# Graph attention layer: queries and values by Strassen's seven products, products that add to a bank behind its reader, softmax later, the end written out

## Chip, cores and metric

One core of a Trainium2 chip. The metric is the device time of one execution in microseconds (us). PE is the matmul engine (TensorE), DVE is VectorE, ACT is ScalarE, SP is the engine that issues DMAs.

## What is computed

The reference passes `x` of 128 graphs x 64 nodes x 256 features (f32) through four layers, each added to its input after a normalisation: graph convolutions with batch normalisation, a spectral layer, graph convolutions with an LSTM over skip windows, and graph attention. The change lies in the fourth. Cut to what matters, with `H` the input after layer normalisation and ReLU:

```
Xq = H @ W_lin.T          # queries, 8192 x 256 by 256 x 256
Xv = H @ W_val.T          # values
e[edge, head] = sum over d of a * leaky_relu(Xq[src] + Xq[dst])  +  log(adj[src, dst] + 1e-8)   # 512 edges, 4 heads, slope 0.2
alpha = softmax of e over the edges that share src
y[src] += alpha * Xv[dst]
out = x + y @ W_out.T
```

## The kernel before

`x` stays in SBUF as 16 blocks `X` of 512 rows (4 row tiles of 128 rows, `TPB`). `layer3` is the fourth layer. It makes 32 steps `g`, each over 4 graphs (half a block); 8 steps form a group that shares one softmax. The tile scheduler decides each engine's order from the order of the code, except in `turn`, where `nc.ordered` fixes it. Every operation goes through a helper, so all have the line L799 in the profile and are told apart by their tiles.

What one step does, in order, and the tiles by which the profile names it:

- `score`: for each of 4 graphs and 2 feature halves a matmul of `Q` (64 rows) with the sum of both edge incidences, `S2` (`ps<-ed_S,Q`), each into one bank; ACT takes it with ReLU into `r` (8 buffers).
- `weighted` of step v-1 (v = g - 10): 16 small matmuls of values `XV` with `an` into `y2`, copied to `y`.
- `reduce`: 8 matmuls of `r` with the attention vector, added into the bank `acc` (`acc<-r,ed_apad`).
- `between` of step v = `spread` (four DVE multiplications of `at` with an edge incidence (`ed_OST`) into `aw`, five buffers) and `gathered` (8 matmuls `ps<-aw,ed_ODT`, copied to `an` by ACT).
- after every eighth step `softmax`: `shifted` first adds the linear part to `acc` by the matmul `acc<-ed_S,lin`, then two scans, a maximum, a subtraction and an exponential (`sm_m`, `sm_e`), then two more scans and a reciprocal on DVE. `edgewise` turns the result into `at` two steps later.
- on odd steps, for the next block, `turned` (normalised `h` by ACT, 8 transposes `ps<-ident,h` into two banks, one copied to `hT` by ACT and one by DVE), then `output`, then `queries`.
- `output` of step v-1: 4 matmuls `ps<-w_o,y`, the residual added by DVE into `X`, and a DMA of 256 KB to `out`.
- in the first eight steps `back` adds transposes `ps<-ident,ls_t` of what the LSTM left.

`queries` multiplies each row tile of `hT` with `WQV`, which holds both weights side by side:

```
for j in range(TPB):
    p = psum.tile([P, BT], F32, name="ps")
    for kc in range(2):
        self.mm(p[:], hT[:, kc, j * P:(j + 1) * P], WQV[:, kc, :], kc == 0, kc == 1)
    self.act(Q[:, j, :], p[:, 0:D], AF.Copy)
    o.copy(V[:, j, :], p[:, D:2 * D])
```

and then forms `lin_p` and its two reductions on DVE. PSUM has five banks named `ps`, one `acc` and two for `y2`. After the 32 steps `turn` holds the last softmax, and a plain loop finishes the last eight `between`, `weighted` and `output`.

Of the kernel before, what the change touches and what calls it, by code (L numbers as in the profile page):

```python
# [8 lines left out]
F32 = mybir.dt.float32  # L9
I32 = mybir.dt.int32  # L10
AF = mybir.ActivationFunctionType
# [12 lines left out]
class Ops:  # L24
# [9 lines left out]
    def add(self, o, a, b):  # L34
        self.tt(o, a, b, ALU.add)
# [807 lines left out]
class Plan:  # L843
# [56 lines left out]
    def rest(self):  # L900

        while any(self.queue.values()):
            for e in self.queue:
                self.fill(e, 1e9)
# [561 lines left out]
class Kernel:  # L1466
# [949 lines left out]
    def layer3(self):  # L2416
        nc, o, io = self.nc, self.o, self.io
        cx, (w,) = self.stage([("l3x", 1)], "tile")
        with cx:
            cy, pools = self.stage([("l3", 2), ("l3v", 2), ("l3s", 1), ("l3r", 6), ("l3ps", 5), ("l3cps", 1), ("l3yps", 1)], "tile")  # L2420
            with cy:
                self.a02 = self.everywhere(w, "ed_a", io["L3_gnn_a"].rearrange("h d -> (h d)"))
                o.ts(self.a02[:], self.a02[:], 0.2, ALU.mult)
                self.drop, self.dropr = (w.tile([P, E], F32, name="ed_" + n) for n in ("drop", "dropr"))
                o.ts(self.drop[:], self.cont[:], 1.0, ALU.subtract, FLOOR, ALU.mult)
                o.ts(self.dropr[:], self.contr[:], 1.0, ALU.subtract, FLOOR, ALU.mult)
                WQV = w.tile([P, 2, 2 * D], F32, name="w3_qv")
                for x, n in enumerate(("W_lin", "W_val")):
                    nc.sync.dma_start(WQV[:, :, x * D:(x + 1) * D],
                                      io[f"L3_gnn_{n}_t"].rearrange("(k p) m -> p k m", p=P))  # L2430
                WO = self.weights(w, "w3_o", io["L3_gnn_W_out_t"])


                st, LAG = {}, 10
                self.turned(st, 0, *pools)
                self.queries(st, 0, WQV, *pools)
                for g in range(8 * NG):
                    v = g - LAG
                    ahead = (g + 1) // 2 if g % 2 and g + 1 < 8 * NG else None
                    self.score(st, g, *pools)  # L2440
                    if v >= 1:
                        self.weighted(st, v - 1, *pools)
                    self.reduce(st, g, *pools)
                    if g % 8 == 1 and 1 < g:
                        self.edgewise(st, g // 8 - 1, *pools)
                    if v >= 0:
                        self.between(st, v, *pools)
                    if g % 8 == 7 and g + 1 < 8 * NG:
                        self.softmax(st, g // 8, *pools)
                    if ahead:  # L2450
                        self.turned(st, ahead, *pools)
                    if g < 8:
                        self.back(8 + g, pools[4], "ps")
                    if g + 6 == 8 * NG:

                        p = pools[4].tile([P, BT], F32, name="ps")
                        for c in range(4):
                            self.nc.tensor.transpose(p[:N, c * P:(c + 1) * P], self.OST[:, c, :], self.ident[:])
                        self.act_copy(self.cont[:N, :], p[:N, :])
                    if v >= 1 and g + 1 < 8 * NG:  # L2460
                        self.output(st, v - 1, WO, *pools)
                    if ahead:
                        self.queries(st, ahead, WQV, *pools)
                self.turn(st, WO, pools)
                for v in range(8 * NG - 8, 8 * NG + 2):
                    if v < 8 * NG:
                        self.between(st, v, *pools)
                    if 8 * NG - 8 < v <= 8 * NG:
                        self.weighted(st, v - 1, *pools)
                    if v > 8 * NG - 7:  # L2470
                        self.output(st, v - 2, WO, *pools)

    def turned(self, st, i, pool, vp, sp, rp, psum, psc, psy):

# [2 lines left out]
        for dc in range(2):  # L2477
# [2 lines left out]
                self.nc.tensor.transpose(p[:, j * P:(j + 1) * P], h[:, j, dc * P:(dc + 1) * P], self.ident[:])  # L2480
            self.move(hT[:, dc, :], p[:])

    def queries(self, st, i, WQV, pool, vp, sp, rp, psum, psc, psy):

        o, hT = self.o, st["hT"]
        Q = rp.tile([P, TPB, D], F32, name="Q", bufs=2)
        V = st["V", i] = rp.tile([P, TPB, D], F32, name="XV", bufs=7)
        st["Q", i] = Q
        for j in range(TPB):
            p = psum.tile([P, BT], F32, name="ps")  # L2490
            for kc in range(2):
                self.mm(p[:], hT[:, kc, j * P:(j + 1) * P], WQV[:, kc, :], kc == 0, kc == 1)
            self.act(Q[:, j, :], p[:, 0:D], AF.Copy)
            o.copy(V[:, j, :], p[:, D:2 * D])

        if i % 4 == 0:
            st["lin", i // 4] = pool.tile([P, 2, 2, 8, HEADS], F32, name="lin")
            self.nc.vector.memset(st["lin", i // 4][:], 0.0)
        lin, pr = st["lin", i // 4], sp.tile([P, TPB, D], F32, name="lin_p")
        o.mul(pr[:], Q[:], self.a02[:, None, :].to_broadcast([P, TPB, D]))  # L2500
        k = 2 * (i % 4)
        for x in range(2):
            s = slice(64 * x, 64 * x + 64)
            o.red(lin[s, x, :, k:k + 2, :].rearrange("p m a h -> p a m h"),
                  pr[s].rearrange("p (a m) (h d) -> p a m h d", m=2, h=HEADS), ALU.add)
# [27 lines left out]
    def turn(self, st, WO, pools):  # L2533


        nc, o, psum = self.nc, self.o, pools[4]
        q, v = NG - 1, 8 * NG - 10
        nc.ordered = True
        W = [self.spread(st, v, c, *pools) for c in (0, 2)]
        e, m, m2 = self.shifted(st, q, *pools)  # L2540
        self.output(st, v - 2, WO, *pools)
        self.gathered(st, v, W, *pools)
        et = m2[:].rearrange("p (c b) -> p c b", c=4)
        p = psum.tile([P, 4, P], F32, name="ps")
        for c in range(4):
            nc.tensor.transpose(p[:, c, :], e[:, c * P:(c + 1) * P], self.ident[:])
        self.act_copy(et, p[:])
        self.weighted(st, v - 1, *pools)
        W = [self.spread(st, v + 1, 0, *pools)]
        p = psum.tile([P, P], F32, name="ps")  # L2550
        for c in range(4):
            self.mm(p[:N, :], self.OST[:, c, :], et[:, c, :], c == 0, c == 3)

        sums = self.contr[:N, 0:P]
        o.ts(sums, p[:N, :], 0.5, ALU.max)
        o.recip(sums, sums)
        self.output(st, v - 1, WO, *pools)
        W.append(self.spread(st, v + 1, 2, *pools))
        self.gathered(st, v + 1, W, *pools)
        at = st["at", q] = pools[1].tile([P, 4, 2, 8, 2, HEADS], F32, name="at")  # L2560
        p = psum.tile([P, 4, P], F32, name="ps")
        for c in range(4):
            self.mm(p[:, c, :], self.cont[:N, c * P:(c + 1) * P], sums)
        for x in range(2):
            for m in range(2):
                z = 64 * x + 32 * m
                by = lambda t: t[:, :, z:z + 32].rearrange("p c (a h) -> p c a h", h=HEADS)
                o.mul(at[:, :, x, :, m, :], by(et), by(p))
        self.weighted(st, v, *pools)
        self.output(st, v, WO, *pools)  # L2570
        self.weighted(st, v + 1, *pools)
        nc.ordered = False
        self.output(st, v + 1, WO, *pools)

    def softmax(self, st, q, pool, vp, sp, rp, psum, psc, psy):

# [7 lines left out]
        o.mul(e[:], e[:], m2[:])  # L2584
        st["e", q] = e

    def shifted(self, st, q, pool, vp, sp, rp, psum, psc, psy):

        nc, o = self.nc, self.o
        acc, lin = st["acc", q], st["lin", q]  # L2590
        self.mm(acc[:], lin[:].rearrange("p x m a h -> p (x m a h)"), self.S2[:], False, True)
        e, m, m2 = (vp.tile([P, E], F32, name="sm_" + x, bufs=1) for x in ("e", "m", "m2"))
        scan = nc.vector.tensor_tensor_scan
        scan(m[:], self.drop[:], acc[:], -FLOOR, op0=ALU.add, op1=ALU.max)
# [58 lines left out]
            (self.move if g < 8 * NG - 11 else self.act_copy)(y[:, :, :, x, :].rearrange("p f m s -> p m f s"),  # L2653
                      yp[:, x, 0:4 * N].rearrange("p (m f s) -> p m f s", m=2, f=2))

    def output(self, st, g, WO, pool, vp, sp, rp, psum, psc, psy):

        y = st["y", g]
        p = psum.tile([P, 2, D], F32, name="ps")
        for m in range(2):  # L2660
            for f in range(2):
                self.mm(p[:, m, :], y[:, f, m].rearrange("p x s -> p (x s)"), WO[:, f, :], f == 0, f == 1)
        x = self.X[g // 2][:, 2 * (g % 2):2 * (g % 2) + 2, :]
        self.o.add(x, x, p[:])
        out = self.io["out"].rearrange("b n d -> (b n) d")
        self.nc.sync.dma_start(out[2 * g * P:(2 * g + 2) * P, :].rearrange("(t p) d -> p t d", p=P), x)

    def run(self):
        self.begin()
# [54 lines left out]
```

## Time and profile before

| | |
|---|---|
| median of 3 runs | 2345.52 us (2345.03 to 2349.55) |
| profiled execution | 2350.61 us, its span 2348.8 us |
| mean granted PE clock | 0.994 of full speed |
| fourth layer in the trace | from about 1750 us to the end |
| PE, DVE, ACT busy | 98%, 68%, 48% of the span |
| largest DMA queue | 7.3% of the time of 16 engines |

The page and the answers of the trace give groups of instructions as engine, operation, out<-in, shape and count, then busy time and mean duration, then idle time ahead of them and what ended it. A matmul of f32 is recorded as two passes. Matmuls overlap in the array, so a group's mean is longer than the distance from one start to the next; distances are taken from the timeline, whose columns are the start, the length, the engine and the group.

### The profile page before, as it was taken

The page shows a single profiled execution, that of the slowest core. Times are in us where ns is not written, and L with a number is a line of the kernel's source. Part 1 is how long each engine was busy: PE and PEld are TensorE (multiplying, and loading weights), DVE is VectorE, ACT ScalarE, POOL GpSimd, SP SyncE. Part 2 cuts the span into 40 slices and gives each one's busy share as a digit, 9 for nine tenths or more (in the row PEclk, how much of TensorE's full clock was granted, in tenths as well). Part 3 has the DMA queues.
Part 4 walks back from the last instruction along what each step waited for, and adds up shares of the span by engine and source line. Part 5 has one row for each costly group of instructions (what it writes and reads, how often), then busy time and mean ns, then how long its engine had stood idle before and what let it go on. Part 6 is the DMA issues. An engine that isn't in the chain of part 4 may idle for free.

```text
span 2348.8 us, 32636 instructions
## 1 busy us (share of the span) xinstructions
PE 2298.7 (98%) x12173; PEld 1633.1 (70%) x12173; DVE 1590.5 (68%) x3988; ACT 1138.2 (48%) x2503; POOL 2.9 (0%) x26
## 2 busy tenths in 40 slices
PE   7999998999999999999999999999999999999999
PEld 4555446986777788888999998888874444444444
DVE  7877676998447777666767667569655566556457
ACT  4665864654436654444444444347445544334321
POOL 0000000000000000000000000000000000000000
PEclk9999999999999999999999999999999999999999
DMA  5000221130010000001000001000020000000001
GB/s 170 1 1 19 63 60 29 66 89 19 1 36 1 1 19 1 1 1 37 1 1 1 1 8 65 1 1 17 1 72 1 1 5 19 14 15 14 19 19 46
DMA packets 61193, 54.86 MB, mean 23 GB/s; under 512 B 15204, under 2 KB 58853, under 8 KB 61029
## 3 DMA queue, kind: packets, MB, share of 16 engines
q1 hardware_dynamic: 61028, 52.73, 7.3%
q8 instruction: 97, 1.59, 0.3%
q14 instruction: 68, 0.55, 0.1%
HBM read 35.93 MB, written 16.78 MB: 22 GB/s over the span
## 4 chain that ended last, share of the span: by engine, by line
PE 80%; DVE 3%; ACT 1%; issue 0%; DMA 0%; ACTq 0%; DVEq 0%
PE ps L799 69%; PE acc L799 5%; PE pt L799 4%; DVE sm_m L799 1%; PE pe L799 1%; PE y L799 1%; DVE X L799 0%; DVE aw L799 0%; ACT ls_g L799 0%; ACT L799 0%; DMA ls_w<-in_L_gnn_Wih_t_dram 0%; DVE ls_g L799 0%; DVE XV L799 0%; DVE ls_t L799 0%; DVE hT L799 0%
## 5 line engine op out<-in xcount | busy, mean ns | idle before, releaser
L799 ACT ACTIVATE ls_g<-ls_g,ls_b 128x512 f32<-128x512 f32 (+4 forms) x472 | 243.0, 565 | 153.4 <-DVE ls_g L799 151.5
L799 ACT ACTIVATE ls_g<-ps,ls_b 128x256 f32<-128x256 f32 (+3 forms) x268 | 115.4, 470 | 330.4 <-PE ps L799 327.1
L799 PE MATMUL ps<-z,w 128*128 128x512 f32 x512 | 259.0, 630 | 0.9 <-ACT z L799 0.9
L799 DVE TENSOR_TENSOR aw<-at,ed_OST 128x1024 f32<-128x1024 f32 x128 | 149.1, 1220 | 97.4 <-PE ps L799 97.4
L799 PE MATMUL ps<-big,X 128*128 128x176 f32 (+3 forms) x848 | 213.0, 367 | 0.8 <-ACT big L799 0.7
L799 DVE TENSOR_TENSOR ls_g<-ls_z,ps 128x512 f32<-128x512 f32 (+5 forms) x256 | 147.1, 580 | 91.4 <-PE ps L799 90.0
L799 PE MATMUL ps<-ls_tx,X 128*128 128x160 f32 (+2 forms) x960 | 207.1, 327 | 0.6 <-ACT ls_g L799 0.6
L799 PE MATMUL ps<-X,X 128*128 128x160 f32 (+1 forms) x896 | 199.1, 306 | 0.0
L799 PE MATMUL ps<-X,ls_w 128*128 128x256 f32 x640 | 190.5, 379 | 0.0
L799 PEld LDWEIGHTS ps<-ls_tx,X 128*128 128x128 f32 x960 | 161.9, 190 | 15.2 <-DVE X L799 4.9
L799 PEld LDWEIGHTS ps<-big,X 128*128 128x128 f32 x848 | 146.1, 190 | 30.5 <-issue 19.4
L799 DVE TENSOR_TENSOR X<-ls_g 128x1024 f32<-128x1024 f32 (+2 forms) x108 | 117.5, 1088 | 51.1 <-ACT ls_g L799 51.1
L799 ACT ACTIVATE r<-ps 128x512 f32<-128x512 f32 x256 | 129.2, 626 | 43.1 <-PE ps L799 43.1
L799 PEld LDWEIGHTS ps<-X,X 128*128 128x128 f32 x896 | 148.5, 190 | 0.0
L799 PE MATMUL ps<-X,ls_s 128*128 128x256 f32 x480 | 142.3, 379 | 0.0
L799 PEld LDWEIGHTS ps<-z,w 128*128 128x128 f32 x512 | 88.7, 193 | 70.9 <-issue 62.3
L799 PE MATMUL ps<-ls_tx,ls_s 128*128 128x256 f32 x464 | 134.9, 379 | 0.0
L799 PE MATMUL ps<-ls_tx,ls_w 128*128 128x256 f32 x464 | 133.4, 380 | 0.0
L799 PEld LDWEIGHTS ps<-X,ls_w 128*128 128x128 f32 x640 | 121.6, 190 | 16.6 <-DVE X L799 0.3
L799 PE MATMUL ps<-big,ls_w 128*128 128x256 f32 x464 | 132.0, 380 | 0.7 <-ACT ls_z L799 0.7
L799 PE MATMUL ps<-ed_S,Q 64*128 64x512 f32 x512 | 129.6, 617 | 2.3 <-DVE XV L799 2.2
L799 ACT ACTIVATE h<-X,n_m,n_r 128x256 f32<-128x256 f32 x192 | 99.6, 590 | 40.9 <-issue 25.0
(543 smaller groups left out, 4010.4 us busy)
## 6 DMA issues: line engine op xcount, KB each, us to landing
X<-in_x_dram SPq DMA_DIRECT2D x32, 512.0 KB
xs<-X SPq DMA_DIRECT2D x16, 512.0 KB
X<-xs SPq DMA_DIRECT2D x16, 512.0 KB
out_dram<-X SPq DMA_DIRECT2D x32, 256.0 KB
X<-in_L_gnn_Wih_t_dram SPq DMA_DIRECT2D x4, 512.0 KB
ls_w<-in_L_gnn_Wih_t_dram SPq DMA_DIRECT2D x4, 512.0 KB
ls_w<-in_L_gnn_Whh_t_dram SPq DMA_DIRECT2D x4, 512.0 KB
w<-in_L_gnn_W_t_dram SPq DMA_DIRECT2D x2, 512.0 KB
```

The lines of the kernel that those rows point to most:

```text
L799: i = method(*a, **kw)
```

## The change

- `queries` multiplies a block of 512 x 256 with the two weights as a 2 x 2 product of 256 x 256 pieces in Strassen's form with seven products (Winograd's variant): each is 2 matmuls of 256 columns. Four stand ahead of `output`, three (`rest`) behind it. Products 2, 4 and 3 have no `start`: they add to the banks a, f and d of products 1, 7 and 5, which by then have been read. `hold` keeps the three behind what PE was given before.
- The outputs are put together by DVE: five additions with an operand in PSUM, and two copies of 512 by ACT.
- `turned` makes three sums (`hS`, one in place in `hT`) right behind the transposes and is moved from the odd step to the even step before; the fourth sum is formed in `queries`. `sums3` makes four sums of the weights once.
- `Q` has one buffer instead of two. The linear part's matmul is a function of its own, `summed`, ahead of the queries; the rest of `softmax` comes after `rest()`.
- In `turn`, `at` is formed ahead of `gathered`, and the last loop is written out in fixed order: half of the next step's `spread` is issued early, the residual additions come a step later (`late`), and the last output goes in two halves, each with its own bank, addition and DMA.

```diff
                 self.turned(st, 0, *pools)
-                self.queries(st, 0, WQV, *pools)
+                WQV = self.sums3(w, WQV)
+                self.queries(st, 0, WQV, *pools)()
...
                     if g % 8 == 7 and g + 1 < 8 * NG:
-                        self.softmax(st, g // 8, *pools)
-                    if ahead:
-                        self.turned(st, ahead, *pools)
+                        self.summed(st, g // 8, *pools)
                     if g < 8:
                         self.back(8 + g, pools[4], "ps")
+                    if ahead:
+                        rest = self.queries(st, ahead, WQV, *pools)
+                    elif g + 2 < 8 * NG:
+                        self.turned(st, g // 2 + 1, *pools)
...
                     if ahead:
-                        self.queries(st, ahead, WQV, *pools)
+                        rest()
+                    if g % 8 == 7 and g + 1 < 8 * NG:
+                        self.softmax(st, g // 8, *pools)
                 self.turn(st, WO, pools)
-                for v in range(8 * NG - 8, 8 * NG + 2):
...
+        A = [[hT[:, k, 256 * t:256 * t + 256] for k in range(2)] for t in range(2)]
+        S = sp.tile([P, 2, 256], F32, name="hS")
+        S1, S2, S3 = A[1][0], S[:, 0], S[:, 1]
+        self.o.sub(S3, A[0][0], A[1][0])
+        self.o.add(S1, A[1][0], A[1][1])
+        self.o.sub(S2, S1, A[0][0])
+        st["sums", i] = A, S1, S2, S3
+
+    def sums3(self, w, WQV):
+        o = self.o
+        B = [[WQV[:, k, D * x:D * x + D] for x in range(2)] for k in range(2)]
+        T1, T2, T3 = (w.tile([P, D], F32, name=f"w3_t{n}")[:] for n in range(3))
+        o.sub(T1, B[1][1], B[0][1])
+        o.sub(B[0][1], B[0][1], B[0][0])
+        o.sub(T2, B[1][1], B[0][1])
+        o.sub(T3, B[1][0], T2)
+        return {1: B[0][0], 2: B[1][0], 3: B[1][1], 5: B[0][1], 7: T1, 6: T2, 4: T3}
...
+        def product(a, m, bank, first):
+            if first:
+                banks[bank] = psum.tile([P, 2, D], F32, name="ps")
+            for u in range(2):
+                nc.tensor.matmul(banks[bank][:, u, :], a[:, u * P:(u + 1) * P], WQV[m], start=first and u == 0,
+                                 stop=u == 1, skip_group_check=True)
+            return banks[bank][:]
+
+        Z, U = V[:, 0:2, :], V[:, 2:4, :]
+        a = product(A[0][0], 1, "a", True)
+        self.act_copy(Z, a)
+        o.add(Z, Z, product(S2, 6, "b", True))
+        o.add(U, Z, product(S3, 7, "f", True))
+
+        o.sub(S3, A[0][1], S2)
+        o.add(U, U, product(S1, 5, "d", True))
+
+        def rest():
+            nc.hold((nc.mark()[0], None, None))
+            self.act_copy(Q[:, 0:2, :], product(A[0][1], 2, "a", False))
+            o.add(Q[:, 2:4, :], Z, product(A[1][1], 4, "f", False))
+            o.add(Z, Z, product(S3, 3, "d", False))
+            nc.hold()
+            self.linear(st, i, pool, vp, sp, rp, psum, psc, psy)
...
         W = [self.spread(st, v, c, *pools) for c in (0, 2)]
+        self.summed(st, q, *pools)
         e, m, m2 = self.shifted(st, q, *pools)
...
-        self.gathered(st, v + 1, W, *pools)
         at = st["at", q] = pools[1].tile([P, 4, 2, 8, 2, HEADS], F32, name="at")
...
+        self.gathered(st, v + 1, W, *pools)
+        W = [self.spread(st, v + 2, 0, *pools)]
         self.weighted(st, v, *pools)
-        self.output(st, v, WO, *pools)
-        self.weighted(st, v + 1, *pools)
+        late = lambda: None
+        for v in range(8 * NG - 8, 8 * NG + 2):
+            if v < 8 * NG:
+                W.append(self.spread(st, v, 2, *pools))
+            late()
+            if v < 8 * NG:
+                self.gathered(st, v, W, *pools)
+            if v + 1 < 8 * NG:
+                W = [self.spread(st, v + 1, 0, *pools)]
+            if v <= 8 * NG:
+                self.weighted(st, v - 1, *pools)
+            late = self.output(st, v - 2, WO, *pools, late=True)
+        late()
         nc.ordered = False
...
+        for lo, hi in ((0, 1), (1, 2)) if g == 8 * NG - 1 else ((0, 2),):
+            p = psum.tile([P, 2, D], F32, name="ps")[:, 0:hi - lo, :]
...
+        def add():
+            for p, lo, hi in parts:
+                x = self.X[g // 2][:, 2 * (g % 2) + lo:2 * (g % 2) + hi, :]
+                self.o.add(x, x, p)
+                self.nc.sync.dma_start(out[(2 * g + lo) * P:(2 * g + hi) * P, :].rearrange("(t p) d -> p t d", p=P), x)
```

More of the change, by code (lines that the diff above doesn't have):

```diff
@@ L2462, in layer3 @@
                     if ahead:
-                        self.queries(st, ahead, WQV, *pools)
+                        rest()
+                    if g % 8 == 7 and g + 1 < 8 * NG:
+                        self.softmax(st, g // 8, *pools)
                 self.turn(st, WO, pools)
-                for v in range(8 * NG - 8, 8 * NG + 2):
[L2466 to L2471, printed above, removed]
     def turned(self, st, i, pool, vp, sp, rp, psum, psc, psy):
@@ L2483, in queries @@
     def queries(self, st, i, WQV, pool, vp, sp, rp, psum, psc, psy):
-        o, hT = self.o, st["hT"]
-        Q = rp.tile([P, TPB, D], F32, name="Q", bufs=2)
+        nc, o, (A, S1, S2, S3) = self.nc, self.o, st["sums", i]
+        Q = st["Q", i] = rp.tile([P, TPB, D], F32, name="Q", bufs=1)
         V = st["V", i] = rp.tile([P, TPB, D], F32, name="XV", bufs=7)
[L2488 to L2494, printed above, removed]
+        banks = {}
@@ new lines, in queries @@
+        o.add(U, Z, product(S3, 7, "f", True))
[8 more added lines that the diff above has]
+            self.linear(st, i, pool, vp, sp, rp, psum, psc, psy)
+        return rest
@@ L2496, in queries, with linear @@
+    def linear(self, st, i, pool, vp, sp, rp, psum, psc, psy):
+        o, Q = self.o, st["Q", i]
         if i % 4 == 0:
@@ L2568, in turn @@
                 o.mul(at[:, :, x, :, m, :], by(et), by(p))
+        self.gathered(st, v + 1, W, *pools)
+        W = [self.spread(st, v + 2, 0, *pools)]
         self.weighted(st, v, *pools)
-        self.output(st, v, WO, *pools)
-        self.weighted(st, v + 1, *pools)
+        late = lambda: None
[11 more added lines that the diff above has]
+        late()
         nc.ordered = False
-        self.output(st, v + 1, WO, *pools)
     def softmax(self, st, q, pool, vp, sp, rp, psum, psc, psy):
@@ L2585, in softmax, with summed @@
         st["e", q] = e
+    def summed(self, st, q, pool, vp, sp, rp, psum, psc, psy):
+        self.mm(st["acc", q][:], st["lin", q][:].rearrange("p x m a h -> p (x m a h)"), self.S2[:], False, True)
     def shifted(self, st, q, pool, vp, sp, rp, psum, psc, psy):
-        nc, o = self.nc, self.o
-        acc, lin = st["acc", q], st["lin", q]
-        self.mm(acc[:], lin[:].rearrange("p x m a h -> p (x m a h)"), self.S2[:], False, True)
+        nc, o, acc = self.nc, self.o, st["acc", q]
         e, m, m2 = (vp.tile([P, E], F32, name="sm_" + x, bufs=1) for x in ("e", "m", "m2"))
@@ L2654, in weighted, with output @@
                       yp[:, x, 0:4 * N].rearrange("p (m f s) -> p m f s", m=2, f=2))
-    def output(self, st, g, WO, pool, vp, sp, rp, psum, psc, psy):
+    def output(self, st, g, WO, pool, vp, sp, rp, psum, psc, psy, late=False):
         y = st["y", g]
[L2659 to L2664, printed above, removed]
-        out = self.io["out"].rearrange("b n d -> (b n) d")
-        self.nc.sync.dma_start(out[2 * g * P:(2 * g + 2) * P, :].rearrange("(t p) d -> p t d", p=P), x)
+        out = self.io["out"].rearrange("b n d -> (b n) d")
+        parts = []
+        for lo, hi in ((0, 1), (1, 2)) if g == 8 * NG - 1 else ((0, 2),):
+            p = psum.tile([P, 2, D], F32, name="ps")[:, 0:hi - lo, :]
+            for m in range(lo, hi):
+                for f in range(2):
+                    self.mm(p[:, m - lo, :], y[:, f, m].rearrange("p x s -> p (x s)"), WO[:, f, :], f == 0, f == 1)
+            parts.append((p, lo, hi))
+        def add():
[3 more added lines that the diff above has]
+                self.nc.sync.dma_start(out[(2 * g + lo) * P:(2 * g + hi) * P, :].rearrange("(t p) d -> p t d", p=P), x)
+        if late:
+            return add
+        add()
     def run(self):
```

## The prediction, made before the result

> **What bounds the kernel now.** I read the page first, then the table by stage, the groups by form from 1750 us on (where the fourth layer begins; it runs to the end at 2348.8, some 597 us), the timelines of a middle step, the waits and the chain.
>
> ```profile
> PE 2298.7 (98%) x12173; PEld 1633.1 (70%) x12173; DVE 1590.5 (68%) x3988; ACT 1138.2 (48%) x2503; POOL 2.9 (0%) x26
> PE 80%; DVE 3%; ACT 1%; issue 0%; DMA 0%; ACTq 0%; DVEq 0%
> ```
>
> PE is busy for 98% of the span and carries 80% of the chain. Busy matmul time alone would not prove that (the Trainium skill, "Trainium Kernel Development and Optimization", warns of it as a metric), so the table by stage follows: time of the stretch, then PE, PEld, DVE, ACT, POOL busy, clock, DMA share, GB/s.
>
> ```profile
> 2050.00:2100.00 50.00, 50.00 (x294) 22.77 (x293) 25.59 (x39) 19.79 (x42) 0.00 (x0) 1.00 0.05 17
> 2250.00:2300.00 50.00, 48.27 (x361) 22.57 (x359) 32.13 (x37) 12.53 (x27) 0.00 (x0) 1.00 0.08 27
> ```
>
> In a middle stretch PE never rests, DVE is half free and ACT 60% free; at the end of the layer PE loses time. So matmul passes taken away count in full as long as DVE and ACT keep up. The groups (busy, mean ns | idle before) and PE's timeline of one odd step give the prices:
>
> ```profile
> L799 PE MATMUL ps<-w_qv,hT 128*128 128x512 f32 x256 | 113.0, 594 | 3.5 <-DVE hT L799 3.5
> L799 PEld LDWEIGHTS ps<-w_qv,hT 128*128 128x128 f32 x256 | 47.7, 190 | 59.3 <-issue 48.5 <-DVE hT L799 5.0 <-PE ps L799 3.3
> L799 DVE TENSOR_TENSOR aw<-at,ed_OST 128x1024 f32<-128x1024 f32 x128 | 149.1, 1220 | 97.4 <-PE ps L799 97.4
> L799 DVE TENSOR_TENSOR X<-X,ps 128x512 f32<-128x512 f32 x48 | 32.2, 682 | 24.9 <-PE ps L799 24.7
> L799 DVE COPY XV<-ps 128x256 f32<-128x256 f32 x64 | 26.5, 416 | 34.1 <-ACT Q L799 34.0
> L799 ACT ACTIVATE Q<-ps 128x256 f32<-128x256 f32 x64 | 24.4, 381 | 62.7 <-PE ps L799 62.3
> L799 ACT ACTIVATE r<-ps 128x512 f32<-128x512 f32 x256 | 129.2, 626 | 43.1 <-PE ps L799 43.1
> ```
> ```profile
> 2237.04 1.09 PE L799 MATMUL ps<-ident,h 128*128 128x128 f32 x8
> 2237.97 1.89 PE L799 MATMUL ps<-w_o,y 128*128 128x256 f32 x8
> 2239.70 7.03 PE L799 MATMUL ps<-w_qv,hT 128*128 128x512 f32 x16
> 2246.66 3.91 PE L799 MATMUL ps<-ed_S,Q 64*128 64x512 f32 x16
> ```
>
> An f32 matmul is two passes. The matmul means overlap, so starts are used: 16 passes of 512 from 2239.70 to 2246.66 are 6.96 us, 0.429 each and 0.09 for the change to the 64-row score. The w_o passes of 256 are 8 in 1.73 us: 0.216 each, exactly half, although a weight load takes 0.190.
>
> **What the Trainium skill says.** "TensorE: Matmul & The Clock Gate", Back-to-back issue gap: spacing in a stream of load and matmul is set by both. The w_o row agrees that at 256 columns the load (0.190) still fits below the pass (0.216), with 0.026 to spare. The same page, What's actually happening: about 3.4 us of idling halves the clock. This trace has it once: a stage at 0.97 (2000 to 2050) after a softmax whose stalls add up. "PSUM — Partial Sum Buffer", The four PSUM rules: a synchronised read in the middle of an accumulation group is allowed, so products that add to a bank behind its reader must wait for the reader; no run here shows that yet.
>
> **The change, part by part.** The sum is against the profiled execution (2350.6, a span of 2348.8 and 1.8 around it). That run is 5.1 above the median of 2345.5; I take the difference in both alike.
>
> 1. Products. Per block of 512 rows 8 matmuls of 512 (16 passes, 6.96) become 14 of 256 (28 x 0.216 + 0.09 = 6.15): -0.81, and x16 blocks **-12.9**. w_o moves between the fourth and the fifth product and ident,h ahead of the w_o of the step before; both change neighbours but not the number of changes between tile shapes, so nothing.
>
> 2. Copies and adds. Three of the sums go with hT into the even step before, where PE wants them only 11 us later; the fourth and the adds follow the products. Per block DVE loses 4 XV copies (1.66) and gains 5 adds out of PSUM (5 x 0.68) and 4 sums of 256 (4 x 0.42): +3.4; ACT goes from 4 x 0.38 to 2 x 0.60. Laid out from the start of an odd score: score 3.9, y 0.6, acc 3.5, aw 3.5, so the products start at +11.5 and the first four end at +15.0, w_o at +16.7. DVE finishes its four aw at about +14.5, then adds: Z +15.2, U +15.9, the last sum +16.3, U +17.0, X +17.7. The fifth product (bank a) waits for ACT alone, the sixth (from +17.6) for U at +15.9, the seventh (from +18.4) for the sum and U at +17.0. About 1.4 us to spare: the adds are hidden by w_o and the fifth and sixth products. If that cover were gone they would cost up to 2.4 a block. Queued behind them on DVE are the adds to Q and Z, lin_p and its two reductions; the next score needs the banks that Q and Z are read from, free by about +20, against its fourth and sixth tiles at that time: margin 0.1. After the even step the sixth score tile waits for the X add, 0 to 0.15: +0.1 x 9 = **+0.9**.
>
> 3. ACT. In blocks 1 to 6 the normalisation (h, four of 0.59) now no longer lies below the 7 us of w_qv, since `turned` comes before w_o of the even step; it mixes with the eight r of the next score, which pace that score's banks (8 r take 4.03 against 3.9 for the matmuls). I read from the order of instructions that an r waits behind one or two h: 0.5 to 0.85 each, **+3.9** for six.
>
> 4. First block. No step runs ahead of it: its sums queue behind the last LSTM work on DVE (ls_g, X, big; done about 1757.9 in the timeline of DVE), and Z and U come after. The block, which ended at 1760.8, ends at about 1763: **+2.3**. The four sums of weights (4 x 0.42) come earlier, below LSTM matmuls: nothing; if they were not covered, +1.7.
>
> 5. Softmax after the queries. The chain stands in softmax passages (here the third):
>
> ```profile
> 2126.66 2.36 DVE aw L799 x2
> 2129.02 2.24 DVE sm_m L799 x2
> 2131.90 2.00 PE ps L799 x4
> ```
>
> and PE's waits say who was late:
>
> ```profile
> PE ps L799 <- DVE hT L799: 3.5, 4, 1.3
> PE ps L799 <- DVE XV L799: 2.2, 3, 0.8
> PE ps L799 <- ACT y L799: 1.6, 2, 0.8
> ```
>
> Today the scans (1.2 each) and a reciprocal (3.34) stand ahead of hT and XV. After, they stand behind the queries on DVE, the exponential with its table load behind the copies on ACT; `softmax` issues no DMA, and its one matmul (`summed`) stays ahead of the queries. In the first softmax I count 2.4 of stalls where 4.5 were: **-2.1**. In the others the score then waits for Q and Z behind the scans, about 2.1 for 2.75 each: **-1.2**. Late next is hT of the following block, behind the reciprocal (1.3 for 0.9, in the sum).
>
> 6. The end. Before, PE waits 1.3 in the aw matmuls at 2282 and 0.85 twice for ACT y, then runs at DVE's pace up to 2303. With at's product ahead of `gathered`, DVE's at is done at about 2286 rather than 2289.4; followed through the aw buffers, the w_o that ended at 2309.6 ends at 2307.4: **-2.2**. The last output in halves: its last add is 0.42 for 0.69 and its transfer half the size, one DMA more on SP's queue, which has 6 us between issues here: **-0.4** (between 0 and -0.8).
>
> Sum: -12.9 + 0.9 + 3.9 + 2.3 - 2.1 - 1.2 - 2.2 - 0.4 = **-11.7**, so 2338.9 for the profiled execution, and 2333.8 from the median.
>
> Unknown costs, both ends: a product that adds to a bank being read, 0 (the fences are met) to 0.3 a block; h among r, 0 to 1.1 a block; the clock after stalls, -1.7 (the half clock of softmax two gone) to +3.3 (two more such); half-width passes in a mixed stream, 0 to +0.01 each (+4.5 in all).
>
> **Rivals.**
> - *All fences are met and the h find gaps.* Without the +3.9 and +0.9, and the clock kept: about -18, 2327.5. For: DVE and ACT are half free. Against: r is paced by ACT at 4.03 for 3.9. Chance 0.15.
> - *DVE becomes the bound of the odd step.* Its queue is in order; where aw begins a microsecond later than I laid out, the sixth and seventh product wait. 0.5 us at 15 blocks is +7.5: 2341.3. For: only 1.4 us to spare. Against: 97 us of idling before aw. 0.14.
> - *Half-width passes are bound by their weight loads.* At 0.245 a pass (28 x 0.245 = 6.9) the products bring nothing: +1, 2346.5. This is also how the change would fail to do what it says. Against: w_o at 0.216. 0.08.
> - *ACT becomes the bound of the even step, and it gets slower.* hT, h and r now meet between the transposes and the score in all 15 blocks, with only w_o's 1.7 us between where 8.7 lay. If the r start behind all four h (2.06 less 0.6 of cover), that is 1.4 x 15 = 21 in place of 3.9: +5.6, 2351. It decides from 1.03 us a block ((11.7 + 3.9) / 15). For: blocks 1 to 6 show that order. Against: from block 7 on the order has h ahead of the r, done 0.1 before the first is wanted. 0.13.
>
> **How the numbers follow.** My own case, -8 to -15 or 2330.5 to 2337.5, has 0.5 and gives the time, 2333.8. The range goes from the good case to beside the half-width one: 2327.0 to 2347.0, leaving out most of the slow rival and the tail of the good one. A measurement here tells 0.2% from no change, 4.7 us. Faster by more than that: my case, most of the good case and 0.1 of the DVE rival, 0.74; within it: half-width and the rest, 0.13; slower: 0.13.
>
> **What would show it.** Right: w_qv with 448 passes starting 0.216 apart; odd steps some 0.8 shorter; no wait for U or Z over 0.2 in the middle; r with 0.5 us waits in the first six blocks; the w_o stretches of the end 2 us earlier. Wrong: PE waiting in each block for DVE XV or hS (the DVE rival), for ACT r after block 6 (the ACT rival), passes further apart than 0.22, or stages with a clock under 1.00 beyond one.

## The result, and the profile after

The changed kernel took 2331.80 us (median of 4 runs, 2327.79 to 2333.19) against 2347.53 for the kernel before (4 runs). The ratio is 0.9926 (95% interval 0.9915 to 0.9938): 15.7 us by the medians, 17 by the ratio. The prediction was 2333.8, range 2327.0 to 2347.0. Its profiled execution took 2327.79 with a span of 2326.0.

The page's first block and its chain, in the order of the lines shown of before:

```profile
PE 2283.2 (98%) x12365; PEld 1664.8 (72%) x12365; DVE 1642.2 (71%) x4073; ACT 1129.4 (49%) x2468; POOL 3.0 (0%) x26
PE 80%; DVE 3%; issue 1%; ACT 0%; ACTq 0%; DVEq 0%
```

PE still bounds the kernel. It has 192 passes more (12 more for each of 16 blocks) and 15.5 us less busy time; DVE has 51.7 us more, which is 3.2 a block. The table by stage (columns as before) shows a middle stretch: PE never rests, DVE is 60% busy.

```profile
2190.00:2240.00 50.00, 50.00 (x315) 25.80 (x313) 29.89 (x36) 17.09 (x34) 0.00 (x0) 1.00 0.05 17
```

PE's timeline of a middle odd step:

```profile
2218.82 1.13 PE L799 MATMUL ps<-w_qv,hT 128*128 128x256 f32 x4
2219.79 1.89 PE L799 MATMUL ps<-w_t,hS 128*128 128x256 f32 x8
2221.52 1.03 PE L799 MATMUL ps<-w_qv,hT 128*128 128x256 f32 x4
2222.38 1.89 PE L799 MATMUL ps<-w_o,y 128*128 128x256 f32 x8
2224.11 1.03 PE L799 MATMUL ps<-w_qv,hT 128*128 128x256 f32 x4
2224.97 1.03 PE L799 MATMUL ps<-w_t,hT 128*128 128x256 f32 x4
2225.83 1.03 PE L799 MATMUL ps<-w_qv,hS 128*128 128x256 f32 x4
2226.79 3.91 PE L799 MATMUL ps<-ed_S,Q 64*128 64x512 f32 x16
```

`w_t` are the weights' sums, `hS` those of the rows; the products come in the order 1, 6 and 7, 5, then w_o, then 2, 4, 3. From 2218.82 to 2226.79 are 7.97 us; without the 1.73 of w_o they are 6.24: 26 passes at 0.216 and the two at a change of shape, 0.32 and 0.31. Products 2, 4 and 3 start with no gap although they add to banks that have just been read. For 4 and 3 DVE's timeline shows it (the pair of XV additions frees banks f and d by 2224.16, ahead of 2224.97 and 2225.83):

```profile
2221.76 0.68 DVE L799 TENSOR_TENSOR XV<-XV,ps 128x512 f32<-128x512 f32 x1
2222.36 0.42 DVE L799 TENSOR_TENSOR hS<-hT,hS 128x256 f32<-128x256 f32 x1
2222.69 1.47 DVE L799 TENSOR_TENSOR XV<-XV,ps 128x512 f32<-128x512 f32 x2
2224.31 0.69 DVE L799 TENSOR_TENSOR X<-X,ps 128x512 f32<-128x512 f32 x1
2226.03 0.69 DVE L799 TENSOR_TENSOR Q<-XV,ps 128x512 f32<-128x512 f32 x1 [1.04 <-PE ps L799]
```

PE's waits in the layer (engine, what it waited for, us in total, times, longest) are 4.1 us for 8.1 before, and of another kind:

```profile
PE ps L799 <- DVE hS L799: 1.6, 1, 1.6
PE ps L799 <- DVE XV L799: 1.0, 3, 0.3
PE ps L799 <- DVE ls_g L799: 0.8, 1, 0.8
PE ps L799 <- DVE hT L799: 0.7, 1, 0.7
```

**How I compare.** Over thirteen traces the layer began anywhere between 1743.1 and 1751.6 us, although hardly anything ahead of it was meant to differ (the four sums of weights, zeros in runs 6 and 7); two traces of the one changed kernel are 8.5 apart (1743.08 and 1751.54); so a span carries several us that the change did not make. From the layer's first transposes (`ident,h`) to the end of the span the traces agree much better: most steps, from one `acc<-r,ed_apad` to the next, repeat within 0.02 us. Below, "layer" is that time: 597.2 before, 582.9 after. Each of these two traces has one stretch at half clock: before, 1.64 us in step 17; after, 2.65 in the first block, both measured against like stretches at full clock. Without them it is 595.5 and 580.3, which a second trace of the changed kernel gave directly (580.26): **-15.2**. Step g is the stretch that ends at the reduce of g, so step 16 holds the softmax that g = 15 calls. Steps are taken in pairs, because moving `turned` shifts 0.82 us of transposes from one step of a pair into the other (13.47 and 21.10 before, 14.29 and 19.45 changed, in steps 19 and 20). Times in us:

| | before | changed | difference |
|---|---|---|---|
| first block | 12.98 | 14.43 | +1.45 |
| steps 1 and 2 (3 and 4, 5 and 6 alike) | 24.70 | 24.85 | +0.15 |
| steps 7 to 10, first softmax | 54.49 | 52.84 | -1.65 |
| steps 11 and 12 | 33.12 | 32.98 | -0.14 |
| steps 19 and 20 (six other plain pairs alike, 17 and 18 without the half clock) | 34.57 | 33.75 | -0.82 |
| steps 15 and 16, second softmax (third alike) | 39.67 | 36.31 | -3.36 |
| from the reduce of 31 to the end | 84.23 | 81.28 | -2.95 |

### The profile page after: what moved, and what is told of

It is laid out like the page before. It is cut to its first block, busy times and chain, and to the rows that moved or that the text cites. A ratio compares the mean times of both kernels' runs of the same rounds, so it can differ in the third digit from the quotient of the medians.

```text
span 2326.0 us, 33145 instructions
## 1 busy us (share of the span) xinstructions
PE 2283.2 (98%) x12365; PEld 1664.8 (72%) x12365; DVE 1642.2 (71%) x4073; ACT 1129.4 (49%) x2468; POOL 3.0 (0%) x26
## 4 chain that ended last, share of the span: by engine, by line
PE 80%; DVE 3%; issue 1%; ACT 0%; ACTq 0%; DVEq 0%
PE ps L799 69%; PE acc L799 5%; PE pt L799 4%; PE pe L799 1%; PE y L799 1%; DVE X L799 1%; DVE aw L799 1%; DVE sm_m L799 0%; DVE XV L799 0%; ACT ls_g L799 0%; DVE ls_g L799 0%; DVE ls_t L799 0%; DVE sm_e L799 0%; DVE lin L799 0%; DVE Q L799 0%
## 5 line engine op out<-in xcount | busy, mean ns | idle before, releaser
L799 PEld LDWEIGHTS ps<-ls_tx,X 128*128 128x128 f32 x960 | 161.8, 190 | 15.2 <-DVE X L799 4.9
```

The lines of the kernel that those rows point to most:

```text
L799: i = method(*a, **kw)
```

## Experiments

Medians come from runs beside the kernel before on the same chip; the ratio is given with its interval. The theory is that of the prediction, corrected by the table; the rival of each run stands in its expectation.

**1. The old end** (e1_old_end).

```diff
+        self.gathered(st, v + 1, W, *pools)
         at = st["at", q] = pools[1].tile([P, 4, 2, 8, 2, HEADS], F32, name="at")
...
-        self.gathered(st, v + 1, W, *pools)
-        W = [self.spread(st, v + 2, 0, *pools)]
         self.weighted(st, v, *pools)
...
+        self.output(st, v, WO, *pools)
+        self.weighted(st, v + 1, *pools)
...
+                for v in range(8 * NG - 8, 8 * NG + 2):
+                    if v < 8 * NG:
+                        self.between(st, v, *pools)
...
-        for lo, hi in ((0, 1), (1, 2)) if g == 8 * NG - 1 else ((0, 2),):
+        for lo, hi in ((0, 2),):
```

> The changed kernel with the end of before: turn in its old order, then the plain loop (between, weighted, output), last output undivided. I read the fourth layer in the trace, from its first transposes (ident,h) to the end of the span: 597.2 us before, 582.9 changed. Theory (the written-out end is worth what the two traces show from score 31 on): 585.8, that is +2.9, with two waits of 0.85 for ACT y and aw at DVE's pace again. Rival (the end is faster only because of what precedes it): within 0.5 of 582.9.

Measured: 2333.16, ratio 0.9931 (0.9915 to 0.9948). Layer 583.28, and it had no half clock, so the comparison is 580.3: **+3.0**, all of it from the reduce of 31 on (84.22 for 81.28). The steps ahead of it are those of the changed kernel within 0.02, so the end's gain is its own. How it divides among the end's edits (`at` earlier, the `spread` by halves, the late additions, the divided output) was not run apart. A part of it is seen in PE's timelines; before:

```profile
2287.24 1.16 PE L799 MATMUL ps<-ed_contr,ed_cont 64*128 64x128 f32 x8
2288.32 0.69 PE L799 MATMUL y<-an,XV 64*64 64x64 f32 x32
2289.79 1.99 PE L799 MATMUL ps<-w_o,y 128*128 128x256 f32 x8 [0.78 <-ACT y L799]
2291.72 0.69 PE L799 MATMUL y<-an,XV 64*64 64x64 f32 x32
2293.19 2.00 PE L799 MATMUL ps<-w_o,y 128*128 128x256 f32 x8 [0.78 <-ACT y L799]
```

and after, where at's product comes ahead of aw, and aw stands between `y` and `w_o`, so that the y copy is covered:

```profile
2262.39 1.16 PE L799 MATMUL ps<-ed_contr,ed_cont 64*128 64x128 f32 x8
2263.47 3.97 PE L799 MATMUL ps<-aw,ed_ODT 128*64 128x512 f32 x16
2267.37 0.69 PE L799 MATMUL y<-an,XV 64*64 64x64 f32 x32
2267.99 4.78 PE L799 MATMUL ps<-aw,ed_ODT 128*64 128x512 f32 x16
```

**2. Softmax ahead of the queries** (e2_softmax_early).

```diff
                         self.summed(st, g // 8, *pools)
+                        self.softmax(st, g // 8, *pools)
...
                         rest()
-                    if g % 8 == 7 and g + 1 < 8 * NG:
-                        self.softmax(st, g // 8, *pools)
```

> The changed kernel with softmax called right behind summed, ahead of the queries. Theory (its scans and reciprocal on DVE hold up the additions of the block): +1.7 at each of the three softmaxes, 588 for the layer, with PE waiting for DVE XV at steps 7, 15 and 23. Rival (softmax gets cheaper because the queries now start early, wherever softmax is called): under +1.5 in all.

Measured: 2335.07, ratio 0.9935 (0.9919 to 0.9952); layer 582.88 against 580.3, **+2.6**: +0.82 at the first softmax, +0.72 at each of the others, +0.28 in step 21 (steps 9 and 10 exchange 0.6). Half of what was expected: between theory and rival. Calling softmax later is a small part of what a softmax step gained. In the changed kernel DVE does not take the softmax as one block behind the queries: at the second softmax the additions of the products and the operations of the softmax come in turn.

```profile
1980.59 0.68 DVE L799 TENSOR_TENSOR XV<-XV,ps 128x512 f32<-128x512 f32 x1
1981.18 0.69 DVE L799 TENSOR_TENSOR sm_m<-sm_m,sm_m 128x512 f32<-128x512 f32 x1
1981.79 0.68 DVE L799 TENSOR_TENSOR XV<-XV,ps 128x512 f32<-128x512 f32 x1
1982.38 0.69 DVE L799 TENSOR_TENSOR sm_e<-acc,sm_m 128x512 f32<-128x512 f32 x1
```

**3. Plain products** (e3_plain_products): all else of the change stays.

```diff
+            def whole():
+                for j in range(TPB):
+                    p = psum.tile([P, BT], F32, name="ps")
+                    for kc in range(2):
+                        self.mm(p[:], st["plain", i][:, kc, j * P:(j + 1) * P], WQV[0][:, kc, :], kc == 0, kc == 1)
+                    self.act(Q[:, j, :], p[:, 0:D], AF.Copy)
+                    o.copy(V[:, j, :], p[:, D:2 * D])
+                self.linear(st, i, pool, vp, sp, rp, psum, psc, psy)
+            return whole
```

> The changed kernel with the eight plain matmuls of 512 a block (and their Q and XV copies) behind w_o, no sums; turned one step early, softmax late and the new end stay. Theory (14 matmuls of 256 save 0.81 a block, and the first block loses 4.1 by its sums): 12.9 - 4.1 = +8.8, 591.7 for the layer; the steps 2, 4 and 6 keep their 4.9 us scores, since those come from turned. Rival (the gain is mostly the moved steps): under +4.

Measured: 2338.66, ratio 0.9951 (0.9935 to 0.9968); layer 589.72, **+9.4** against 580.3. The plain pairs of steps are +0.82, the softmax steps only +0.17 (22.18 for 22.01), step 17 +1.5 (a wait for r, see run 9), and the first block -1.45. Steps 7 to 10, around the first softmax, are 52.81 for 52.84. So the seven products are worth 0.82 in a plain pair, 0.17 at the later softmaxes and nothing at the first. That DVE, busy with the scans, is what takes the rest fits run 6, where one more addition on DVE is free in a plain step and costs 0.6 at a softmax. The nearness of 9.4 to the 8.8 expected is partly chance: 2.65 of the 4.1 booked for the first block was half clock. And with plain products the softmax steps are still 22.18, when before has 26.20: of these 4 us 0.82 are the transposes, which now lie in the step before, and the rest has another cause than the products.

**4. Plain products in the first block alone** (e4_first_plain).

```diff
+        if i == 0:
+            st["plain", i] = hT
+            st["sums", i] = None, None, None, None
+            return
         A = [[hT[:, k, 256 * t:256 * t + 256] for k in range(2)] for t in range(2)]
```

> The changed kernel with plain products in the first block alone (the weights' sums then take a fourth small tile). Theory (the 2.0 us wait for hS behind the LSTM's last DVE work, and half clock after it, are the 4.1 us that the first block lost): about 13.1 from the first transposes to the first reduce instead of 17.1, the clock at 1.00 there, 578.9 for the layer. Rival (the half clock comes from the LSTM's end, which both kernels have): -2 only, with passes at half clock still there.

Measured: 2328.99, ratio 0.9905 (0.9888 to 0.9922); layer 578.89, first block 12.98. The wait for hS is gone from the list. But against an undisturbed first block this is -1.45, not -4.1: the half clock that followed the wait in the first trace was in none of seven later traces with the same block. This is how the block looks in the second trace of the changed kernel:

```profile
1753.62 1.13 PE L799 MATMUL ps<-w_qv,hT 128*128 128x256 f32 x4
1756.38 1.99 PE L799 MATMUL ps<-w_t,hS 128*128 128x256 f32 x8 [1.63 <-DVE hS L799]
1758.21 1.89 PE L799 MATMUL ps<-w_qv,hT 128*128 128x256 f32 x8
```

Product 6, the second to be issued, waits 1.6 us for the sums, as the prediction had it.

**5. All h a step sooner** (e5_norm_early): the first edit is in `turned`, which also takes the `h` made ahead, the second in `queries`.

```diff
+        if i + 1 < NB:
+            st["f", i + 1] = self.factors(pool, *self.moments(pool, i + 1))
...
         self.act_copy(Z, a)
+        if i + 1 < NB:
+            nc.hold((None, None, nc.mark()[2]))
+            st["h", i + 1] = self.norm(pool, i + 1, by=st.pop(("f", i + 1)))
+            nc.hold()
```

> The changed kernel with the four h of the next block issued on ACT right behind the XV copy of the block before (their factors by DVE a step sooner), so that no h stands among the r. I read the layer from its first transposes to the end of the span; without a half clock it is 580.3 changed. Theory (an r behind an h makes the early even scores 4.9 us instead of 3.9): the steps into g = 1, 3, 5, 7 go from 10.4 to 9.4, the one into 11 from 13.5 to 12.6, perhaps 9 as well: 575. Rival (the transposes of ls_t and hT on ACT are what is late, not h): under -2, with the 4.9 us scores still there; or Q is now late behind h, and the odd steps lose what the even ones win.

Measured: 2338.68, ratio 0.9958 (0.9945 to 0.9971): slower than the changed kernel; layer 584.53, +4.3. Two things in one run. The steps into 3, 5, 7 and 11 fell from 10.38 and 13.53 to 9.61 and 12.56: the h among the r make those scores long, for 0.8 of the 1.05 that steps 3, 5 and 7 lose against before (8.51 and 0.82 of transposes). In the changed kernel ACT's timeline reads

```profile
1791.25 0.59 ACT L799 ACTIVATE h<-X,n_m,n_r 128x256 f32<-128x256 f32 x1
1791.74 0.58 ACT L799 ACTIVATE r<-ps 128x512 f32<-128x512 f32 x1
1792.22 0.59 ACT L799 ACTIVATE h<-X,n_m,n_r 128x256 f32<-128x256 f32 x1
1792.71 0.58 ACT L799 ACTIVATE r<-ps 128x512 f32<-128x512 f32 x1
```

and here

```profile
1791.72 0.59 ACT L799 ACTIVATE hT<-ps 128x512 f32<-128x512 f32 x1
1792.63 4.03 ACT L799 ACTIVATE r<-ps 128x512 f32<-128x512 f32 x8 [0.33 <-PE ps L799]
```

But steps 9 and 17 rose by 3.5 and 3.6. Behind a softmax the factors of the next block now queue behind the reciprocal on DVE, ACT waits in order for them with hT and the r behind it, and PE waits for hT:

```profile
1868.51 0.21 ACT L799 ACTIVATE n_y<-n_v 128x4 f32<-128x4 f32 x1 [5.81 <-DVE n_v L799]
1868.62 0.58 ACT L799 ACTIVATE hT<-ps 128x512 f32<-128x512 f32 x1
```

**6 and 7. How much room DVE has** (e6_one_more, e7_three_more): additions of zeros between those to Z and U, one as shown, or `range(3 if i else 0)`.

```diff
+        for _ in range(1 if i else 0):
+            o.add(Z, Z, self.zeros[:].rearrange("p (t d) -> p t d", t=2))
         o.add(U, Z, product(S3, 7, "f", True))
```

> The changed kernel with one more DVE addition of 128x512 (zeros, nothing changes in the result) between the additions to Z and U of each block but the first: 0.68 us later for U. Theory (DVE has 1.4 us to spare in a middle odd step): 0 there, +0.5 at each of the three softmax steps, so +1.5. Rival (DVE already bounds the odd step): +0.68 for 15 blocks, +10.

> As the one before with three more additions, 2.04 us. Theory (1.4 to spare): +0.6 a middle step, +2 at a softmax, +12 in all. Rival (DVE bounds already): +30. A third reading (the spare time is well above 1.4): under +4.

Measured: one more gives a layer of 586.66, +6.4, and 2334.94 (ratio 0.9956, 0.9938 to 0.9974); three more give 607.0, +26.7, and 2355.0 in one run. From step 12 on, one more costs nothing in a middle step (19.45 as before), and 0.6 at the second and third softmax; but +1.6 at step 2 and +1.9 at steps 8 and 10; why those three is not shown. Three more cost 1.70 in every middle step, nearly their whole length. Room between 0.6 and 1.8 us is what this pins down (one addition takes 0.6 from start to start). That the loss then is 1.7 and not the 0.6 that was expected I can't lay to DVE's time alone: with three more the order differs too, the X addition now ahead of those to U, and a score tile between products 2 and 4. For one more the theory said 1.5 and the rival 10, for three 12 and 30: the measured 6.4 and 26.7 lie between, the second nearer the rival. The middle steps are closer to the limit than "1.4 to spare" suggests.

**8. `turned` back in the odd step** (e9_turned_odd).

```diff
                     if ahead:
+                        self.turned(st, ahead, *pools)
                         rest = self.queries(st, ahead, WQV, *pools)
-                    elif g + 2 < 8 * NG:
-                        self.turned(st, g // 2 + 1, *pools)
```

> The changed kernel with turned back in the odd step, right ahead of the queries; products, softmax and end stay. Theory (the sums need the even step to hide: hT on two engines 0.6 to 0.7 after the transposes, three sums of 0.42 behind it, and DVE's aw in front): PE waits about 1.5 to 2.5 a block for hT and hS, while the early scores get their 1.0 back: +20 to +30, 600 to 610, more than the plain products lose. Rival (w_o and the first product cover it): within 5 of the changed kernel.

Measured: 2376.59, ratio 1.0128 (1.0100 to 1.0156): slower than the kernel before. Layer 626.1, +45.9, above the range expected. PE's waits:

```profile
PE ps L799 <- DVE hS L799: 23.1, 14, 3.3
PE ps L799 <- DVE hT L799: 9.0, 11, 1.3
PE ps L799 <- DVE n_r L799: 2.4, 1, 2.4
```

Seven products without the earlier `turned` would have lost (626.1 against 595.5 before). The early odd steps do get their short scores back (8.51).

**9. The kernel before with `turned` alone a step sooner** (e10_before_turned_early).

```diff
-                    if ahead:
-                        self.turned(st, ahead, *pools)
                     if g < 8:
                         self.back(8 + g, pools[4], "ps")
+                    if g % 2 == 0 and g + 2 < 8 * NG:
+                        self.turned(st, g // 2 + 1, *pools)
```

> The kernel before with turned alone moved a step sooner (behind back of the even step), plain products, softmax and end as before. Theory (from the runs with plain products and with the early softmax: of the 4.0 us that a softmax step lost against before, 0.7 are the late softmax, the rest that hT is ready before the scans): about -3 at each of the three softmaxes and +1.0 at each of the six early scores, so 592 for the layer against 595.5. Rival (the late softmax is needed for it): no gain at g = 16 and 24, and the early scores make it slower, 601.

Measured: 2343.82, ratio 0.9979 (0.9968 to 0.9990): faster by this line alone. Layer 592.9 against 595.5, **-2.6**. The second and third softmax steps are 22.31 for 26.20; with the transposes in step 15 counted, steps 15 and 16 are 36.60 for 39.67, so -3.07 of the -3.36 that the whole change gains there. Steps 7 to 10 are 52.81 for 54.49, all that the whole change gains at the first softmax. The early pairs are +1.0 (25.71 for 24.70). Step 17 has +1.5: on ACT a table load of 1.28 stands behind the second of its eight r, and PE waits for the next one; in the changed kernel the load stands behind the third, and PE does not wait. PE's timeline of the second softmax tells why; before:

```profile
1985.04 0.33 PE L799 MATMUL y<-an,XV 64*64 64x64 f32 x4
1986.14 7.13 PE L799 MATMUL ps<-w_qv,hT 128*128 128x512 f32 x16 [0.77 <-DVE hT L799]
1993.21 3.91 PE L799 MATMUL ps<-ed_S,Q 64*128 64x512 f32 x14
1997.85 1.12 PE L799 MATMUL ps<-ed_S,Q 64*128 64x512 f32 x2 [0.73 <-DVE XV L799]
```

and with hT made ahead of the scans:

```profile
1979.87 1.89 PE L799 MATMUL ps<-w_o,y 128*128 128x256 f32 x8
1981.59 7.03 PE L799 MATMUL ps<-w_qv,hT 128*128 128x512 f32 x16
1988.55 4.04 PE L799 MATMUL ps<-ed_S,Q 64*128 64x512 f32 x16
```

Both waits are gone, with the softmax where it was. From start to start they had cost about 1.0 us (1985.04 to 1986.14, for four passes of y) and 1.8 (1993.21 to 1998.90, for a score of 3.9), more than the idle time recorded. PE now reaches the queries early enough for all XV copies to come ahead of the reciprocal on DVE; before the change the last of them stood behind it:

```profile
1994.18 3.33 DVE L799 RECIPROCAL sm_m<-sm_m 128x512 f32<-128x512 f32 x1
1997.43 0.36 DVE L799 COPY XV<-ps 128x256 f32<-128x256 f32 x1
```

and with `turned` a step sooner

```profile
1990.16 0.40 DVE L799 COPY XV<-ps 128x256 f32<-128x256 f32 x1
1990.47 3.34 DVE L799 RECIPROCAL sm_m<-sm_m 128x512 f32<-128x512 f32 x1
```

Runs 9, 1 and 3 together account for the change: `turned` alone -2.6, the new end -2.95, the later softmax under plain products -0.3 (22.18 for 22.31 at two steps), and the seven products on top of these -9.4 (1.5 of it at step 17, where that wait for r is gone). That adds up to the -15.2 measured. The later softmax is worth 2.6 under the seven products (run 2) and 0.3 without them, which fits that it makes room for their additions rather than saving time by itself.

**10 and 11. A version from these, beside the changed kernel again** (e8_both, e11_changed): the first block plain, and the h of blocks 2 to 5 early; the first condition stands at both edits of run 5.

```diff
-        if i + 1 < NB:
+        if i + 1 < 5:
...
             self.act_copy(Q[:, 0:2, :], product(A[0][1], 2, "a", False))
+            if i == 3:
+                nc.hold((nc.mark()[0], None, nc.mark()[2]))
+                st["h", 5] = self.norm(pool, 5, by=st.pop(("f", 5)))
...
```

> The changed kernel with plain products in the first block, and the h of blocks 2 to 5 issued early: those of 2 to 4 behind the XV copy of the block before, those of 5 behind the Q copy of block 3, where ACT rests. From block 6 on the h stay where they were, since early factors made the steps after a softmax wait for hT (+3.5 at g = 9 and 17 in the run with all of them early). Theory: -1.5 from the first block, -0.4 at g = 1, -0.8 at g = 3 and 5, some 0.5 lost between: 577 for the layer against 580.3, 3 us less than the changed kernel. Rival (the wait only moves to the Q copy or the next r): the first block's 1.5 alone, 579.

> The changed kernel again, on the same chip as the two others, as their comparison. If the half clock in the first block of its first trace is chance (four later kernels with the same first block did not have it), 580.3 for the layer; else 582.9.

Measured: the version 2327.58, ratio 0.9914 (0.9900 to 0.9928), layer 577.62; the changed kernel 2333.66, ratio 0.9934 (0.9921 to 0.9948), layer 580.26. The layer is **2.7** shorter, the first block's 1.45, 1.0 at step 1 and about 0.8 at each of steps 3 and 5, but +1.05 at step 7. There block 6's h still stands among the r, so the score stays long (4.98 for 4.96 in the changed kernel); the loss comes ahead of it, in the reduce, which takes 4.69 for 3.65: on ACT its last r stand behind two tiny operations of the early factors (`n_y`), which wait 1.37 and 0.53 for DVE. The intervals of the two ratios overlap a little; the steps don't.

## Why the prediction was right, and where its steps were not

The prediction said -11.7; the layer without half clocks says -15.2, the medians -15.7. The direction, the mechanism of the products and most terms held. That the time, 2331.80, came so near to 2333.8 is in part luck: the kernel before ran 2.0 slower beside the changed one (2347.53) than in the runs that the sum started from, and the difference itself lies just beyond the -8 to -15 of the main case. By its own steps:

1. **Products, -0.81 a block.** Held in the seven plain pairs, at -0.82. A pass of 256 stayed at 0.216 beside its 0.190 load; the section Back-to-back issue gap of the Trainium skill's "TensorE: Matmul & The Clock Gate" says that the load and the matmul together set the spacing, and here the longer of the two was the pass. The rival of half-width passes is out. It did not hold "x16": at the softmaxes the products bring 0.17 and 0 (run 3).
2. **Adds hidden.** Held: the middle steps show no wait, so the +0.9 did not come. Adding to a bank behind its reader costs a product nothing here; the synchronised read that the Trainium skill's "PSUM — Partial Sum Buffer" allows (The four PSUM rules) is now seen in a trace. The rival with DVE as bound is out, but narrowly (runs 6 and 7).
3. **h among the r, +3.9.** Mechanism right (run 5), size low: about 1.0 a score in steps 1, 3, 5 and 7 rather than 0.65. Steps 1 to 6 show +1.0 a pair in run 9, where nothing else changed. The ACT rival, which took it into all 15 blocks, is out: in the middle steps the score stays at 3.90.
4. **First block, +2.3.** The wait is where it was put. The block lost 1.45 in a usual trace and 4.1 in the first. The 2.3 was the block's end against its end before, with the products' saving in it already, so it was 0.85 too high; but step 1 booked -0.81 for this block again. That the net of the two, +1.5, is what the block lost is luck.
5. **Softmax, -2.1 and -1.2.** The step that failed. I counted on 2.1 of waits being left in the second and third softmax of 2.75 before, and gave what was saved to the later softmax call. Measured: steps 15 and 16 have -3.36, as have 23 and 24, where steps 1 and 5 of the sum come to -0.81 and -0.6. Run 9 shows -3.07 of it for `turned` alone, which the prediction costed only by the adds (item 2) and the h (item 3): hT is now made ahead of the scans on DVE, and the XV copies ahead of the reciprocal. PE still waits 0.3 for XV, which is all that is left of the 2.1, since DVE takes the softmax and the additions in turn (run 2), where I had put them in one block. At the first softmax steps 7 to 10 have -1.65, where the sum had about -2.4 (two blocks' products, two scores of +0.65, -2.1); there too run 9 has it all, and the products bring nothing.
6. **The end, -2.6.** Held: -2.95, and run 1 shows it to be its own. Up to the start of the last y it is -2.2, as put; behind it, with the divided output, -0.75 for the -0.4.

So 3.9 us of the gain were missed at two softmaxes, 0.9 in item 2 and 0.35 at the end, against about 1 too little loss in item 3 (steps 1 to 6) and 0.8 at the first softmax; the named unknown of a half clock (-1.7 in the trace of before) was there, and hit the first trace of after with +2.65 instead.

## What to carry to other kernels

When a step is moved, look at what it passes on every queue, not only at what it meets at its new place: here the move that was only meant to hide some sums took the transposes past the softmax scans on DVE and gained there, by itself, what the softmax's own move was credited with. Fewer matmul passes counted in full only in steps where the engine that puts the results together had room; the same seven products were worth 0.82 us in a plain pair of steps, 0.17 or nothing at a softmax and less than nothing in the first block, so use them where they pay. Compare stretches between the same two instructions rather than spans when the parts ahead of the change vary by more than the change itself.

## What the runs showed of the hardware that I had not expected

Half clock did not follow from the wait alone. The same 1.6 us wait for hS was followed in one trace of eight by 13 passes 0.427 apart, some 5.5 us (the table by stage has a clock of 0.66 from 1745 to 1755), and by full speed in the others. In the kernel before the second and the third softmax have the same waits, 0.77 and 0.73, and half clock followed the second alone. The prediction took the idling of about 3.4 us that the Trainium skill names ("TensorE: Matmul & The Clock Gate", What's actually happening) as the condition, and the second softmax as a case of it; but no wait that long stands in these stretches, and what set the half clock off stays open. The start of the layer moved by 8.5 us between two executions of the same kernel, also for a reason that is not shown, while steps inside it repeated to 0.02.
